# Separate step lists for sequences 0, 1 and 15 of a two-layer transformer kernel

## The chip, the cores and the metric

The kernel runs on one core of a Trainium2 chip. The core has five engines that work side by side and meet at semaphores: TensorE (PE, with its weight loads shown apart as PEld), VectorE (DVE), ScalarE (ACT), GpSimd (POOL) and SyncE (SP, which issues most of the DMAs here). The metric is the device time of one execution in microseconds.

## The reference, cut to what matters

The input is 16 sequences of 512 tokens with 256 channels. Two layers follow each other, each of an attention part and a feed-forward part, with a layernorm after each part.

- Layer 0, attention: queries, keys and values of 16 heads are mapped into latents of 32, rotated (rope), scored with a causal mask, put through a softmax, and weighted sums of the value latents go through two projections.
- Layer 0, feed-forward: inputs, hidden values and weights are quantized to FP4 in blocks of 16 and back; the form is silu(gate) * up, then down, with 704 hidden channels.
- Layer 1, attention: a recurrence over the 512 time steps, `state = tanh(state @ tanh(a) + x_t @ b)`, for all sequences at once.
- Layer 1, feed-forward: a gate and a squared relu of mixes of a token with the one before it.

```python
x = _layernorm(x + _L0_attn_ref(x, ...), axis=-1)
x = _layernorm(x + _L0_ffn_ref(x, ...), axis=-1)
x = _layernorm(x + _L1_attn_ref(x, ...), axis=-1)
x = _layernorm(x + _L1_ffn_ref(x, ...), axis=-1)
```

## The kernel before, in words

After a short preparation the kernel goes through the 16 sequences of layer 0 one after another (loop at L779). The recurrence of layer 1 needs all of them and comes last (L1118 and after).

**Slots.** A sequence is cut into 12 slots: 4 groups `g` of four heads by 3 blocks `n` of query rows. A slot issues the scores of four heads (`scores`, L516: matmuls into the four tiles `S`, then a masked pass on DVE that writes `p` and its extreme `nm`), and, for the slot before, four turns (`turn`, L555: transposes of `p` into `ps_pt`, copied by ACT to `pT`); the exponentials (`exponentials`, L544, ACT) run two heads behind. After a group's third block, `weighted` (L566) issues the 80 matmuls of `py`. In the second of a slot's four rounds `divide` (L597) turns the reciprocal sums (`ps_r`, copied to `rT`) and multiplies them into `yT`.

**Steps beside the scores.** All other work of layer 0 is cut into steps. A slot has eight half-slots, one before and one after each of its four turns, and each half-slot may issue some steps. An entry of the list `PLAN` (L632) such as `"U-1.2"` names a task, a sequence relative to the current one, and a part:

- `H` (L433): queries and keys of the heads, four steps per sequence. `V` (L415): values, two steps.
- `L` (L446): latents of one group, three steps: plain products (`ps_q`, `ps_k`), rotated ones (`ps_qs`, `ps_ks`), and the product `ps_qf` that ends in `qr`, which the scores read.
- `O` (L482): output projection, residual and layernorm, two steps. It waits until the last group of its sequence is divided.
- `Q` (L272): puts the quantization of 128 tokens into a queue whose pieces are issued one per half-slot (`vector_step`, L257), or at once when a step needs the result. The quantization (`fp4`, L181) is some nine DVE instructions and two on POOL, ending in `xq` or `hq`.
- `U` (L282): gate and up products of 128 tokens, three steps. The first transposes `xq` (`ps_xq`, copied to `xqT`); the other two are the products `pg` and `pu` and the silu. The last one queues the quantization of the hidden values.
- `D` (L313): down product of 128 tokens, two steps: transposes of `hq` (`ps_h`, copied by ACT to `hT`), and twelve matmuls into `ps_d` with residual, layernorm and the store.
- `W` (L217): quantizing and transposing the feed-forward weights, 30 steps, only beside sequence 0. `P`: a pause, which counts 0.5 of time and issues nothing.

`Beside` (L670) paces a list: the sum of `TIME` over its entries is spread evenly over the sequence's 96 half-slots, and an entry is issued when the credit is positive. A task is a generator, so an entry means "the next step of this task"; `"U-1.3"` in one list and `"U-2.3"` in the next go on with the same task.

**What sets the order.** PE's order is the program's, written by hand (`manual_schedule`). The instructions of DVE, ACT and POOL are ordered by a planner when the kernel is built; it may place an instruction before or after others of its engine as soon as its inputs and buffers are free by its own estimate, with the program's order as priority.[...]

**Buffers that matter below.** Two pools of PSUM banks (two and five) serve `S`, turns and steps; `py` has one bank. `hT`, `qc`, `qs` and `ks` have one buffer each; `xq`, `hq`, `xqT`, the quantization's scratch and the residual `x` have two.

**The lists before.** There is one list, `PLAN`. `plan(b)` (L647) drops entries whose sequence lies outside 0 to 15; at the last sequence it adds the leftovers of sequence 14 at the end; at sequence 0 it puts in the two `V` steps and spreads the 30 `W` steps over the rest of the list. After the last slot a list `FIRST` (L1085) does sequence 15's own feed-forward.

Of the kernel before, what the change touches and what calls it, by code (L numbers as in the profile page):

```python
# [19 lines left out]
P = 128  # L20
B, T, C = 16, 512, 256
NT = T // P
H, HD, L = 16, 16, 32
# [36 lines left out]
def tile_kernel(ctx: ExitStack, tc: tile.TileContext, I: dict, out: bass.AP):  # L60
# [87 lines left out]
    def mm(name):  # L148
        banks.append(banks.pop(0))
        return banks[-1].tile([P, 512], F32, tag="mm", name=name)  # L150
# [21 lines left out]
    def whole_steps(pieces):  # L172

        t = 0.0
        for dt, end in pieces:
            t += dt
            if end:
                yield t
                t = 0.0

    def fp4(dst, x, nb, rows=P):  # L181

        n = nb * 16
        sc = ffn.tile([P, 44], F32, tag="q_sc", name="q_sc", bufs=2)[:rows, :nb]  # L190
        inv = ffn.tile([P, 44], F32, tag="q_inv", name="q_inv", bufs=2)[:rows, :nb]
        q = ffn.tile([P, FF], F32, tag="q_q", name="q_q", bufs=2)[:rows, :n]
        m = ffn.tile([P, FF], F32, tag="q_m", name="q_m", bufs=2)[:rows, :n]

        def blocks(t):
            return t.rearrange("p (n k) -> p n k", k=16)

        def over(t):
            return t.unsqueeze(2).to_broadcast([rows, nb, 16])

        nc.vector.tensor_reduce(sc, blocks(x), AX.X, ALU.max, apply_absolute_value=True)
        nc.vector.tensor_scalar(sc, sc, 1.0 / 6.0, 1e-12, ALU.mult, ALU.max)
        nc.vector.reciprocal(inv, sc)
        nc.vector.tensor_scalar(inv, inv, 1.0 - 2.0**-23, None, ALU.mult)
        if n > C:
            yield
        nc.vector.tensor_tensor(blocks(q), blocks(x), over(inv), ALU.mult)
        yield
        nc.vector.tensor_scalar(m.bitcast(U32), q.bitcast(U32), 0x7F800000, None, ALU.bitwise_and)
        nc.vector.tensor_scalar(m, m, 1.0, 1.5 * 2.0**22, ALU.max, ALU.mult)  # L210
        if n > C:
            yield
        nc.vector.tensor_tensor(q, q, m, ALU.add)  # L213
        nc.gpsimd.tensor_tensor(q, q, m, ALU.subtract)  # L214
        nc.gpsimd.tensor_tensor(blocks(dst), blocks(q), over(sc), ALU.mult)

    def ffn_weights():  # L217

        for name, dst in (("w_gate", wgT), ("w_up", wuT)):
            for r in range(NFB):  # L220
                n = min(P, FF - r * P)
                w = ffn.tile([P, C], F32, tag="h", name="w", bufs=2)
                nc.sync.dma_start(w[:n, :], I[name][r * P : r * P + n, :])
                wq4 = ffn.tile([P, C], F32, tag="hq", name="wq4", bufs=2)
                for _ in fp4(wq4[:n, :], w[:n, :], C // 16, n):
                    pass
                yield 0.3
                ps = mm("ps_t")
                for cc in range(2):
                    nc.tensor.transpose(  # L230
                        ps[:, cc * P : cc * P + n], wq4[:n, cc * P : cc * P + P], ident[:n, :n]
                    )
                nc.scalar.copy(
                    dst[:, :, r * P : r * P + n],
                    ps[:, : 2 * P].rearrange("p (c n) -> p c n", c=2)[:, :, :n],
                )
                yield 1.2
        for r in range(2):
            w = ffn.tile([P, FF], F32, tag="h", name="w", bufs=2)
            nc.sync.dma_start(w, I["w_down"][r * P : r * P + P, :])  # L240
            wq4 = ffn.tile([P, FF], F32, tag="hq", name="wq4", bufs=2)
            for _ in fp4(wq4, w, FF // 16):
                pass
            yield 0.3
            for k0 in (0, 3):
                ps = mm("ps_t")
                for kb in range(k0, k0 + 3):
                    (of, n), at = PARTS[kb], (kb - k0) * P
                    nc.tensor.transpose(ps[:n, at : at + P], wq4[:, of : of + n], ident)
                    nc.scalar.copy(wdT[:n, kb, r * P : r * P + P], ps[:n, at : at + P])  # L250
                yield 1.5
# [30 lines left out]
    def ffn_up(b, j):  # L282
        vector_done(("x", b, j))
        xq = xq_of.pop((b, j))
        ps = mm("ps_xq")
        for cc in range(2):
            nc.tensor.transpose(ps[:, cc * P : cc * P + P], xq[:, cc * P : cc * P + P], ident)
        xqT = ffn.tile([P, 2, P], F32, tag="xqT", name="xqT", bufs=2)
        copier[0](xqT.rearrange("p c t -> p (c t)"), ps[:, : 2 * P])  # L289
        yield 0.3, True  # L290
        h = ffn.tile([P, FF], F32, tag="h", name="h", bufs=2)
        for f in range(2):
            fs = slice(f * 352, f * 352 + 352)

            th = ffn.tile([P, 352], F32, tag="th", name="th", bufs=2)
            for w in (wgT, wuT):
                ps = mm("pg" if w is wgT else "pu")
                for cc in range(2):
                    product_of[0](ps[:, :352], xqT[:, cc, :], w[:, cc, fs], cc == 0, cc == 1)
                    if cc == 0:  # L300
                        yield 0.6, False
                if w is wgT:
                    nc.scalar.activation(th, ps[:, :352], AF.Tanh, scale=0.5)
                    nc.vector.scalar_tensor_tensor(th, th, 1.0, ps[:, :352], ALU.add, ALU.mult)
                    yield 0.6, False
                else:
                    nc.vector.scalar_tensor_tensor(h[:, fs], th, 0.5, ps[:, :352], ALU.mult, ALU.mult)
            if f == 1:
                hq_of[b, j] = hq = ffn.tile([P, FF], F32, tag="hq", name="hq", bufs=2)
                queue(("h", b, j), fp4(hq, h, FF // 16))  # L310
            yield 0.6, True
# [29 lines left out]
    with ExitStack() as a:  # L341
# [44 lines left out]
        for i in range(2):  # L386
            nc.gpsimd.tensor_copy(bd["bdqs"][:, i::2], bd["bdq"][:, 1 - i :: 2])
            at = COLS["q2lb"][0]
# [3 lines left out]
        for i in range(2):  # L392
            at = COLS["cab"][0] + 2
# [222 lines left out]
        def pause(b):  # L616
# [10 lines left out]
        TASKS = {  # L627
            "L": latents, "H": heads, "V": values, "O": out_projection, "Q": quantize,
            "U": lambda b, j: whole_steps(ffn_up(b, j)), "D": lambda b, j: whole_steps(ffn_down(b, j)),
            "W": ffn_weights, "P": pause,  # L630
        }
        PLAN = [  # L632
            "L0.1", "L0.1", "U-2.3", "U-2.3", "H0", "H0", "O-1", "D-2.2", "L0.1", "D-2.2", "O-1",
            "V1", "L0.2", "L0.2", "L0.3", "Q-1.0", "L0.3", "Q-1.1", "U-1.0", "L0.2", "D-2.3",
            "U-1.1", "U-1.0", "U-1.0", "V1", "L0.3", "U-1.1", "Q-1.2", "H1", "U-1.2", "D-2.3",
            "Q-1.3", "U-1.2", "U-1.1", "U-1.2", "H1", "U-1.3", "D-1.0", "D-1.0", "D-1.1", "L1.0",
            "L1.0", "D-1.1", "L1.0",
        ]
        tasks = {}

# [5 lines left out]

        def plan(b):  # L647
            todo = []
            for entry in PLAN:
                c, *rest = entry[1:].split(".")  # L650
                c = b + int(c)
                if 0 <= c < B:
                    todo.append((entry[0], (c, *map(int, rest))))
            if b == B - 1:

                todo += [(e[0], (b - 1, int(e[-1]))) for e in PLAN if e[1:3] == "-2"]
            if b == 0:

                todo[2:2] = [("V", (0,))] * 2
                first = todo.index(("L", (0, 2))) + 3  # L660
                n = len(todo) - first
                for k in reversed(range(n)):
                    at = first + k + 1
                    todo[at:at] = [("W", ())] * ((k + 1) * 30 // n - k * 30 // n)
            return todo


# [2 lines left out]
        class Beside:  # L670
            def __init__(self, b):
                self.todo = plan(b)
                self.pace = sum(TIME[n] for n, _ in self.todo) / (4 * len(BLOCKS) * 8)
                self.left = 0.0
# [104 lines left out]
        with tc.manual_schedule(engines={mybir.EngineType.PE}):  # L779
# [4 lines left out]
            for slot in slots + [None]:  # L784
                if slot:
                    b, g, n = slot
# [281 lines left out]
    def beside(M):  # L1068

        todo = [("N", 1)] * 2 if M == 0 else []  # L1070
        for e in PERIOD:
            i = M + int(e[1:])
            if 0 <= i < T // TS:
                todo.append((e[0], i))
        return todo + LATER.get(M, [])
# [42 lines left out]
    with tc.manual_schedule(engines={mybir.EngineType.PE}):  # L1118
# [33 lines left out]
        todo, left, pace = [], 0.0, 0.0  # L1152
# [7 lines left out]
        for t in range(T):  # L1160
            if t % 16 == 0:
                for e in todo:
                    step(*e)
                todo, left = beside(t // 16), 0.0
# [5 lines left out]
            for g in range(2):  # L1170
                if us[g] is None or us[g][0] + us[g][1] == t:
                    t0, n = starts[g].pop(0)
# [6 lines left out]
            if t % 8 == 7:  # L1179
                at = t % 16 - 7  # L1180
# [113 lines left out]
```

## Time and profile before

| | |
|---|---|
| median of three runs | 2609.86 us (2609.65 to 2614.08) |
| the profiled execution | 2613.92 us, span 2612.1 us, mean granted PE clock 0.979 |
| busy, share of the span | PE 94%, PEld 66%, DVE 75%, ACT 62%, POOL 40% |
| first scores of sequence 0, 1, 2 | 32.6, 136.4, 259.7 us |
| one of sequences 2 to 14 | 107.5 to 109.0 us |
| first and last scores of sequence 15 | 1664.5, 1785.0 us |
| first step of the recurrence | 1864.4 us |

In rows of waits "PE ps_d L160 <- ACT hT L323: 2.7, 1, 2.7" means: PE stood still before an instruction of line 160 that writes `ps_d`, until ACT's instruction of line 323 on `hT` was done; 2.7 us in total, once, 2.7 at the longest. PE counts as busy while a matmul is on its way, so a small wait within a group of matmuls can hide there.

### The profile page before, as it was taken

The numbers are of one execution on the slowest core, as the hardware profiler recorded it, in microseconds if no ns is written. First come the engines' busy times: TensorE is split into PE (matmuls) and PEld (weight loads), VectorE is DVE, ScalarE is ACT, GpSimd is POOL, SyncE is SP. The second block draws the span as 40 slices with busy tenths as digits, with TensorE's granted clock in tenths as the row PEclk, the third lists the DMA queues.
The fourth block names the chain that finished last, engine by engine and source line by source line (L and its number), as shares of the span: only waits on it lengthen the run. The fifth ranks groups of instructions, "written<-read, shape, count | busy, mean of one in ns | idle before, by whom it ended". The sixth has DMA issues, their size and how long they took to land.

```text
span 2612.1 us, 73864 instructions
## 1 busy us (share of the span) xinstructions
PE 2451.8 (94%) x28802; PEld 1725.3 (66%) x28802; DVE 1946.2 (75%) x5621; ACT 1613.5 (62%) x5532; POOL 1044.0 (40%) x1649
## 2 busy tenths in 40 slices
PE   7788999999999999999999999987799999999997
PEld 4455666666666666666666666655577777777775
DVE  5865888788887888878888788875656666666665
ACT  4655666666766666666666666653266666666663
POOL 4322333333333333333333333333545555555553
PEclk9899999999999999999999999998899999999999
DMA  3000000000000000000000000000111111111100
GB/s 114 23 9 5 11 23 14 15 15 11 23 13 15 15 11 23 14 15 15 12 23 14 16 15 6 15 11 9 42 31 39 39 37 37 39 40 39 35 27 22
DMA packets 58016, 61.30 MB, mean 23 GB/s; under 512 B 7873, under 2 KB 53058, under 8 KB 57666
## 3 DMA queue, kind: packets, MB, share of 16 engines
q1 hardware_dynamic: 56802, 55.54, 6.9%
q8 instruction: 226, 3.70, 0.6%
q10 hardware_dynamic: 864, 1.05, 0.1%
q14 instruction: 124, 1.02, 0.1%
HBM read 39.79 MB, written 16.78 MB: 22 GB/s over the span
## 4 chain that ended last, share of the span: by engine, by line
PE 53%; DVE 30%; ACT 7%; POOL 4%; issue 4%; DMA 1%; SPq 1%; ACTq 0%; POOLq 0%; DVEq 0%
PE u L1053 7%; PE ps_pt L559 5%; DVE p L536 5%; PE S L524 5%; PE u L1013 4%; PE pg L160 3%; PE pu L160 3%; ACT p L549 3%; PE ps_d L160 3%; PE ps_h L439 3%; PE py L590 2%; PE ps_a L897 2%; PE ps_k L897 2%; PE ps_rr L897 2%; DVE q_q L213 2%
## 5 line engine op out<-in xcount | busy, mean ns | idle before, releaser
L549 ACT ACTIVATE p<-p,nm 128x512 f32<-128x512 f32 (+3 forms) x1024 | 569.4, 561 | 522.4 <-DVE nm L536 518.3
L1061 ACT ACTIVATE hist<-u 64x64 f32<-64x64 f32 x2048 | 445.6, 218 | 253.0 <-PE u L1053 183.3
L536 DVE CUSTOM_DVE_ANT_0 p<-S,mask 128x512 f32<-128x512 f32 (+3 forms) x1024 | 442.7, 483 | 71.5 <-PE S L524 71.4
L559 PEld LDWEIGHTS ps_pt<-ident,p 128*128 128x128 f32 x2560 | 299.0, 142 | 232.9 <-issue 89.1
L1053 PEld LDWEIGHTS u<-hist,ta 128*64 128x64 f32 x8176 | 363.3, 138 | 121.0 <-ACT hist L1061 41.7
L561 ACT COPY pT<-ps_pt 128x384 f32<-128x384 f32 (+1 forms) x768 | 370.9, 514 | 72.4 <-PE ps_pt L559 72.4
L559 PE MATMUL ps_pt<-ident,p 128*128 128x128 f32 x2560 | 394.0, 280 | 8.4 <-DVE nm L536 4.6
L1053 PE MATMUL u<-hist,ta 128*64 128x32 f32 x8176 | 384.5, 219 | 4.8 <-ACT hist L1061 4.6
L214 POOL TENSOR_TENSOR q_q<-q_q,q_m 128x256 f32<-128x256 f32 (+1 forms) x142 | 167.9, 1183 | 491.8 <-DVE q_q L213 486.7
L524 PE MATMUL S<-kc,qr 32*128 32x128 f32 (+3 forms) x2048 | 238.1, 474 | 11.6 <-ACT qr L478 9.5
L1013 PE MATMUL u<-xt,wb 128*64 128x64 f32 x4128 | 223.4, 230 | 3.5 <-issue 2.4
L549 ACT ACTIVATION_READ_ACCUMULATOR p<-p,nm 128x1 f32 x1024 | 198.5, 194 | 0.0
L160 PE MATMUL ps_d<-wdT,hT 128*128 128x256 f32 x732 | 180.2, 398 | 7.4 <-ACT hT L323 6.2
L160 PE MATMUL pg<-wgT,xqT 128*128 128x352 f32 x512 | 177.3, 469 | 7.9 <-ACT xqT L289 4.7
L160 PE MATMUL pu<-wuT,xqT 128*128 128x352 f32 x512 | 174.8, 464 | 0.0
L473 POOL TENSOR_TENSOR qc<-qc,qs 128x512 f32<-128x512 f32 x64 | 81.6, 1275 | 226.0 <-DVE qs L472 210.8
L1013 PEld LDWEIGHTS u<-xt,wb 128*64 128x64 f32 x4128 | 165.2, 139 | 9.2 <-issue 3.0
L590 PEld LDWEIGHTS py<-pT,vpad 128*32 128x32 f32 x5120 | 138.6, 110 | 39.7 <-issue 32.1
L524 PEld LDWEIGHTS S<-kc,qr 32*128 32x128 f32 x2048 | 111.0, 184 | 79.0 <-issue 37.1
L590 PE MATMUL py<-pT,vpad 128*32 128x128 f32 x5120 | 160.5, 274 | 2.7 <-ACT pT L561 2.4
L160 PEld LDWEIGHTS ps_d<-wdT,hT 128*128 128x128 f32 x732 | 141.5, 200 | 30.4 <-ACT hT L323 11.5
L1187 POOL COPY c<-hist 64x256 f32<-64x256 f32 x256 | 111.3, 435 | 65.6 <-ACT hist L1061 56.1
(164 smaller groups left out, 4536.0 us busy)
## 6 DMA issues: line engine op xcount, KB each, us to landing
xT<-in_xT_dram SPq DMA_DIRECT2D x16, 512.0 KB
x<-in_x_dram SPq DMA_DIRECT2D x16, 512.0 KB
xs<-x SPq DMA_DIRECT2D x64, 128.0 KB
x<-xs SPq DMA_DIRECT2D x32, 256.0 KB
xm<-xs SPq DMA_DIRECT2D x32, 256.0 KB
out_dram<-o SPq DMA_DIRECT2D x64, 128.0 KB
w<-in_w_down_dram SPq DMA_DIRECT2D x2, 352.0 KB
w<-in_w_gate_dram SPq DMA_DIRECT2D x5, 128.0 KB
```

The lines of the kernel that those rows point to most:

```text
L160: nc.tensor.matmul(dst, left, right, start=start, stop=stop)
L214: nc.gpsimd.tensor_tensor(q, q, m, ALU.subtract)
L524: nc.tensor.matmul(S[h][:, at : at + w], q[rs, i * P : i * P + P], k[rs, :w], start=True, stop=True,)
L536: nc.vector.tensor_tensor_reduce(out=p[:, own], in0=S[h][:, own], in1=mask[:, T - (i + 1) * P :], scale=1.0, scalar=-MASKED, op0=ALU.add, ...
L549: nc.scalar.activation(p[:, own], p[:, own], AF.Exp, bias=nm[:, u : u + 1], scale=-1.0, accum_out=sum_of[b, g][:, cb, half, h : h + 1],)
L559: nc.tensor.transpose(ps[:, at : at + P], p[:, at : at + P], ident)
L561: nc.scalar.copy(pT[:, :w], ps[:, :w])
L590: nc.tensor.matmul(py[q * 32 : q * 32 + 32, PLACE[i][1], :], vpad[b % 2][:, j, g * 4 + h, :], pt, start=j == 0 and h % 2 == 0, stop=j == i ...
L897: nc.tensor.matmul(dst[cs], left[:, cs], right, start=first, stop=not first)
L1013: nc.tensor.matmul(u[rs, k, par:n:2, bs : bs + 16], wb[:, g * 2 + k, par, half, rs], xt[:, g, at : at + n - par : 2, :], start=par == 0 an ...
L1053: nc.tensor.matmul(into[cs, :, c, :], ta[:, t % 2, g * 2 + k, cs], own[:, :, c, :], start=False, stop=True, skip_group_check=True,)
L1061: nc.scalar.activation(state[g][rs, :, r * 32 : r * 32 + 32].rearrange("p k (s b) -> p k s b", s=2), u[rs, :, t - t0, :] .rearrange("p k ( ...
```

## The change

The middle list keeps its entries; four of its steps change places. Sequences 0, 1 and 15 get lists of their own, so `plan` no longer drops or adds anything. The new lists hold the same steps as before, in another order, plus one pause in the lists of 0 and 1 and five in that of 15. Some `D` and `U` steps of sequences 13 and 14 beside sequence 15 now interleave with each other.

```diff
-            "W": ffn_weights, "P": pause,
+            "W": lambda b: ffn_weights(), "P": pause,
         }
         PLAN = [
-            "L0.1", "L0.1", "U-2.3", "U-2.3", "H0", "H0", "O-1", "D-2.2", "L0.1", "D-2.2", "O-1",
-            "V1", "L0.2", "L0.2", "L0.3", "Q-1.0", "L0.3", "Q-1.1", "U-1.0", "L0.2", "D-2.3",
+            "L0.1", "L0.1", "U-2.3", "U-2.3", "H0", "H0", "O-1", "D-2.2", "L0.1", "O-1", "V1",
+            "D-2.2", "L0.2", "L0.2", "L0.3", "Q-1.0", "L0.3", "Q-1.1", "L0.2", "U-1.0", "D-2.3",
             "U-1.1", "U-1.0", "U-1.0", "V1", "L0.3", "U-1.1", "Q-1.2", "H1", "U-1.2", "D-2.3",
             "Q-1.3", "U-1.2", "U-1.1", "U-1.2", "H1", "U-1.3", "D-1.0", "D-1.0", "D-1.1", "L1.0",
             "L1.0", "D-1.1", "L1.0",
         ]
+        PLAN_0 = [
+            "H0", "L0.1", "H0", "V0", "V0", "L0.1", "L0.2", "W0", "V1", "L0.1", "L0.2", "V1",
+            "L0.3", "L0.2", "W0", "L0.3", "W0", "W0", "W0", "H1", "L0.3", "W0", "W0", "W0", "H1",
+            "W0", "W0", "W0", "W0", "W0", "W0", "W0", "L1.0", "W0", "W0", "W0", "W0", "L1.0", "W0",
+            "W0", "W0", "W0", "W0", "W0", "L1.0", "W0", "W0", "W0", "W0", "W0", "P0",
+        ]
+        PLAN_1 = [
+            "H0", "H0", "L0.1", "L0.1", "O-1", "O-1", "L0.1", "L0.2", "L0.2", "Q-1.1", "V1", "L0.3",
+            "Q-1.0", "U-1.0", "U-1.1", "U-1.0", "P0", "U-1.0", "V1", "L0.2", "L0.3", "U-1.1",
+            "Q-1.2", "U-1.1", "U-1.2", "L0.3", "D-1.0", "H1", "Q-1.3", "H1", "L1.0", "D-1.0",
+            "U-1.2", "L1.0", "D-1.1", "U-1.2", "U-1.3", "L1.0", "D-1.1",
+        ]
+        PLAN_15 = [
+            "L0.1", "U-2.3", "U-2.3", "H0", "H0", "L0.1", "O-1", "D-2.2", "L0.1", "P0", "D-2.3",
+            "L0.2", "D-2.2", "L0.3", "L0.2", "O-1", "Q-1.0", "U-1.0", "L0.2", "L0.3", "U-1.0", "P0",
+            "P0", "Q-1.1", "U-1.0", "L0.3", "U-1.1", "U-1.1", "D-2.3", "Q-1.2", "Q-1.3", "P0",
+            "U-1.2", "D-1.0", "U-1.3", "U-1.2", "P0", "U-1.1", "U-1.2", "D-1.0", "U-1.3", "U-1.3",
+            "D-1.1", "D-1.1", "D-1.3", "D-1.2", "D-1.3", "D-1.2",
+        ]
...
-            for entry in PLAN:
+            for entry in {0: PLAN_0, 1: PLAN_1, B - 1: PLAN_15}.get(b, PLAN):
                 c, *rest = entry[1:].split(".")
-                c = b + int(c)
-                if 0 <= c < B:
-                    todo.append((entry[0], (c, *map(int, rest))))
-            if b == B - 1:
-
-                todo += [(e[0], (b - 1, int(e[-1]))) for e in PLAN if e[1:3] == "-2"]
-            if b == 0:
-
-                todo[2:2] = [("V", (0,))] * 2
-                first = todo.index(("L", (0, 2))) + 3
-                n = len(todo) - first
-                for k in reversed(range(n)):
-                    at = first + k + 1
-                    todo[at:at] = [("W", ())] * ((k + 1) * 30 // n - k * 30 // n)
+                todo.append((entry[0], (b + int(c), *map(int, rest))))
             return todo
```

## Prediction

> **What bounds the kernel now.** I read the slices of the page first, then busy times by stage, then who TensorE waits for in each stage, and last single instructions at the longest stalls.
>
> ```profile
> ## 2 busy tenths in 40 slices
> PE   7788999999999999999999999987799999999997
> ...
> PEclk9899999999999999999999999998899999999999
> ```
>
> TensorE (PE) is full nearly everywhere. The holes are at both ends of the attention part: slices 0 to 3 and 26 to 28. PEclk dips where PE has holes. I cut the span at the first score matmul of sequences 0, 1, 2, 4, 5, 15 and at the end of the scores:
>
> ```profile
> 32.60:136.40 103.80, 85.71 (x647) 51.13 (x647) 72.81 (x235) 69.29 (x215) 33.61 (x40) 0.89 0.12 35
> 136.40:259.70 123.30, 102.40 (x799) 65.16 (x798) 77.18 (x245) 67.32 (x196) 29.50 (x34) 0.95 0.02 8
> 259.70:367.20 107.50, 105.74 (x848) 70.85 (x848) 88.50 (x266) 73.25 (x224) 37.55 (x45) 1.00 0.05 15
> 475.20:583.00 107.80, 105.84 (x848) 70.91 (x849) 88.94 (x266) 70.95 (x213) 37.25 (x45) 1.00 0.05 16
> 1664.50:1785.00 120.50, 104.86 (x825) 70.66 (x825) 84.68 (x251) 65.56 (x190) 34.48 (x42) 0.94 0.04 11
> 1785.00:1864.40 79.40, 52.35 (x326) 36.78 (x324) 54.10 (x142) 15.12 (x45) 32.30 (x42) 0.83 0.07 22
> ```
>
> The columns are the length, then busy PE, PEld, DVE, ACT, POOL, and the clock. A middle sequence takes 107.5 to 109.0 us with PE idle for about 2: PE sets the pace, at full clock. Sequence 1 has fewer matmuls (799 against 848) and takes 123.3 us, 20.9 of them idle; sequence 15 takes 120.5 with 15.6 idle; sequence 0 takes 103.8 with 18.1 idle and 647 matmuls. No engine is full there. So these three are bound by the order of the list: PE meets a step whose input is still being made. The longest such waits of PE in sequence 0, in 1, and in 15 to its last step:
>
> ```profile
> PE ps_t L249 <- POOL wq L215: 4.8, 1, 4.8
> PE ps_t L249 <- ACT wdT L250: 4.7, 8, 1.5
> PE ps_pt L559 <- DVE nm L536: 3.1, 1, 3.1
> ```
>
> ```profile
> PE pg L160 <- ACT xqT L289: 3.2, 1, 3.2
> PE pg L160 <- DVE nm L536: 3.2, 1, 3.2
> PE ps_d L160 <- ACT hT L323: 2.7, 1, 2.7
> PE ps_o L491 <- DVE yT L611: 2.6, 1, 2.6
> ```
>
> ```profile
> PE ps_xq L287 <- POOL xq L215: 7.2, 1, 7.2
> PE ps_h L321 <- POOL hq L215: 4.0, 1, 4.0
> PE ps_d L160 <- ACT hT L323: 3.3, 1, 3.3
> ```
>
> The timeline of the 4.0 us shows what a quantization costs from end to end:
>
> ```profile
> 1784.09 0.89 DVE L201 TENSOR_REDUCE q_sc<-h 128x44 f32<-128x704 f32 x1
> ...
> 1789.23 1.68 POOL L214 TENSOR_TENSOR q_q<-q_q,q_m 128x704 f32<-128x704 f32 x1 [15.54 <-DVE q_q L213]
> ...
> 1790.99 1.38 POOL L215 TENSOR_TENSOR hq<-q_q,q_sc 128x704 f32<-128x704 f32 x1
> ...
> 1792.43 1.54 PE L321 MATMUL ps_h<-ident,hq 128*128 128x128 f32 x6 [3.95 <-POOL hq L215]
> ```
>
> From 1784.09 to 1792.37 is 8.3 us on DVE and POOL; PE had too little between to cover it.
>
> **What the Trainium skill says.** "TensorE: Matmul & The Clock Gate", Part 1 (the HAM clock gate): PE drops to half clock after an idle window of about 3.4 us and needs a busy one to recover. The trace agrees: four `pg` matmuls take 1.35 us at 1744.7 and 2.71 us at 1819.3, behind a stall of 10.2 us. So a stall costs itself plus slow matmuls behind it. The same page, Architectural detail, says that ACT and DVE are strictly first in, first out[...]; the trace agrees at 1710 to 1714, where DVE sits 3.3 us in front of `yT` although a ready quantization stands behind it. The page "PSUM — Partial Sum Buffer", Specifications (TRN2), gives eight banks; the code spends two and five of them on scores, turns and steps and one on `py`. That they can run out is seen below, at `ps_k`.
>
> **The change part by part.** I place steps by walking each list at its pace (sum of TIME over 96 half-slots) and write slot.half, so 6.2 is slot 6, half-slot 2. A half-slot is 1.1 to 1.3 us (a stage's length over 96). No instruction is added or removed: PE, DVE, ACT, POOL and DMA work are the same, and a pause issues nothing. Issues on SP follow their steps; DMA is 2 to 12% busy in these stages, nothing on the path. Only what stands between a producer and its reader moves. The planner lets DVE, ACT and POOL run ahead of a step's place (the first quantization of a weight starts at 14.5 us, long before its place in slot 3), so mostly PE's place of the reader counts.
>
> *Sequence 15.* (a) `U14.2`'s transpose goes from 6.2 to 6.7, five half-slots, at the middle's 1.12 us 5.6 us of other work: the 7.2 becomes about 2; -5. (b) The last part of `U14.3` goes from 10.3 to 9.6, its `D` from 11.4 to 10.7. The distance stays nine half-slots, but they now hold the second half of `D14.1` (12 matmuls, 2.7), `py` (2.3), sixteen transposes (2.2), the scores (0.9) and 1.6 of other transposes: 9.7 against the chain of 8.3, with up to 3.6 us of DVE's other work mixed in (four score passes of 0.55, one layernorm of 1.4): -2.5. (c) The two halves of `D14.1` go from neighbours (9.1, 9.2) to 10.2, 10.3 with about 1 us of transposes between: -1. (d) DVE's lateness around slot 8 (1.6 + 1.0 + 0.4): -1. (e) Half clock fills 20 us here; with half of that gone, at 70% busy, 10 x 0.5 x 0.7 = 3.5; I take -2.5. (f) New: `D13.3` begins (2.4) before `D13.2` ends (2.7), and `D14.2` before `D14.3`, on the single buffer `hT`: the copy (0.87) waits for 12 matmuls; +1 each, and +1 for its bank. Sum -9, bounds -16 and +5.
>
> *Sequence 1.* (a) `U0.2`'s transpose and first product, at 6.5 and 6.6, part to 6.4 and 8.7: -3.2. (b) `D0.0`'s halves, 9.1 and 9.2, part to 6.7 and 8.1: -2.7. (c) `L1.2` and `L1.3`, packed into 2.2 to 3.3 (waits of 1.3 and 1.1), spread to 6.5: -2. (d) `L2.0` ends at 10.5 instead of 11.3: the next scores' 1.6 falls to the middle's 0.5; -1. (e) Waits on `nm` (3.2, 1.1, 1.0) are DVE's lateness; -1. (f) 12.5 us of half clock shrink; -2. (g) `O0` stays right behind the division: 0. (h) New: `U0.0`'s transpose and product become neighbours (3.0, 3.1), where such neighbours cost 3.2 above; +2. `L1.3` starts at 2.6, but its `qc` (one buffer) is free only when `L1.2` ends, at 4.6 instead of 3.3: a bank is held some 11 half-slots longer; +1. Sum -9, bounds -17 and +6.
>
> *Sequence 0.* (a) Quantization of `w_down` and its transposes, both at 10.0, go to 9.7 and 10.1: 4.8 falls by 3 half-slots at most; -2. (b) `wdT` (4.7) is a transpose waiting for the copy of the one before in its bank: 0. (c) The `L` steps spread from slot 2 (eight pairs) over slots 1 to 4, the weights in slot 5 thin out: the 3.1 and the slow scores in slots 3 and 6 (2.7 and 2.1 against 1.1 us); -3. (d) Clock, 21.9 us at half: -1. Sum -6, bounds -13 and +5.
>
> *Sequences 2 to 14.* `O`'s second half goes from 3.2 to 2.5, `V` from 3.4 to 2.7, `D-2.2`'s second half from 2.5 to 3.1, `U-1.0`'s transpose from 4.3 to 4.5, `L.2`'s end from 4.4 to 4.3. In slot 3 `ps_o` held its bank from 505.8 to 509.2 behind DVE's four score passes and `ps_k` started 0.8 late. That 0.8 goes; slot 2 becomes fuller, +0.5. -0.3 x 13 = -4, bounds -1.5 and +3 each (-20 and +39). `U-1.0`'s copy is covered by six transposes of `D-2.3`, two turns and two more transposes, some 2.3 us.
>
> After 1785 us nothing moves; the end of sequence 15 only shifts it. Sum: -9 - 9 - 6 - 4 = -28. The profiled execution took 2613.92 us (span 2612.1 and 1.8 around it), the median of the runs is 4 us lower: 2609.86 - 28 = **2582**.
>
> **Rivals.** *A middle list that waits* (slower). ACT takes `xqT`'s copy late because exponentials ahead of it wait for DVE: ACT waits 418 us for `nm` in the middle. `U-1.0`'s product then stands as in sequence 1, 3.2 us. It counts thirteen times: from 24 / 13 = 1.8 us per sequence the gain of the three lists is used up; 3.2 gives 2609.86 - 24 + 42 = 2628. Against it: the cover of 2.3 us. *Stalls that move* (no change): DVE and ACT are ordered anew by the planner, and what one stall loses the next regains, as the old list's `D` and `U` of sequence 15 queue for the same DVE; 2605 to 2615. *All to the floor* (faster still): without idle time and half clock sequence 15 would take about 105, 1 about 106, 0 about 92: -15 - 17 - 12 - 4 = -48: 2562. For it: besides PE no engine is over 71% busy there. Against it: DVE and ACT must then never be late.
>
> **How the numbers follow.** Forecast 0.53 (own range 2566 to 2598), floor 0.16, no change 0.12, waiting middle 0.19. Within 0.2% (5 us) is about what a measurement of this kernel can't tell from no change. Faster 0.69, same 0.12, slower 0.19. From 2552 to 2626 the range takes the forecast, no change, most of the floor and half of the slower case.
>
> **What would show it.** Right: sequences 0, 1 and 15 at about 98, 114 and 112 us by the first scores; `ps_xq <- xq` in 15 under 3 us, `pg <- xqT` and `ps_d <- hT` gone from 1; fewer half-clock windows; a middle sequence at 107.3. Wrong: a middle sequence over 109 us with a new row in PE's waits, or `xq` and `hq` waits of the old size at new places.

## The result, and the profile after

The changed kernel takes 2582.46 us (median; 2580.31 to 2582.77), beside 2611.97 us for the kernel before, measured together: ratio 0.9884, 95% interval 0.9867 to 0.9901, about 30 us faster. The profiled execution has a span of 2581.0 us (before 2612.1) and a mean PE clock of 0.983 (before 0.979).

The slices of the page after, busy tenths and granted clock:

```profile
PE   8789999999999999999999999996899999999997
PEclk9899999999999999999999999998899999999999
```

The hole of three slices behind sequence 15 has become two; the first slices have hardly changed. The windows of the kernel after, cut at the same places (first scores of sequences 0, 1, 2; of 4 and 5; first and last of 15; first step of the recurrence). Columns: length, then busy PE, PEld, DVE, ACT, POOL, the clock, DMA:

```profile
31.55:130.30 98.75, 82.52 (x650) 51.10 (x650) 69.83 (x234) 68.62 (x213) 34.19 (x39) 0.90 0.12 37
130.30:241.40 111.10, 99.06 (x798) 63.71 (x797) 76.68 (x239) 65.33 (x194) 29.60 (x34) 0.95 0.02 8
458.00:566.00 108.00, 105.98 (x848) 70.78 (x849) 89.11 (x266) 71.07 (x213) 37.46 (x45) 1.00 0.05 16
1652.10:1762.50 110.40, 100.29 (x825) 66.76 (x826) 88.16 (x259) 65.48 (x190) 37.12 (x44) 0.98 0.03 11
1762.50:1833.60 71.10, 47.36 (x322) 33.34 (x322) 50.62 (x136) 14.69 (x45) 29.23 (x40) 0.88 0.08 27
```

Beside the windows of before, with the whole middle (sequences 2 to 14) from its first to its last first score:

| stage | before | after | difference | foretold |
|---|---|---|---|---|
| start, to the first scores | 32.6 | 31.6 | -1.0 | 0 |
| sequence 0 | 103.8 | 98.7 | -5.1 | -6 |
| sequence 1 | 123.3 | 111.1 | -12.2 | -9 |
| sequences 2 to 14 | 1404.8 | 1410.7 | **+5.9** | -4 |
| sequence 15 to its last scores | 120.5 | 110.4 | -10.1 | -9, with the next row |
| from there to the recurrence | 79.4 | 71.1 | -8.3 | |
| recurrence and after | 747.7 | 747.3 | -0.4 | 0 |

So the forecast met the time while one of its terms had the wrong sign and another was half of what came: the middle became slower by 5.9 where -4 stood, and sequence 15 with what follows gained 18.4 where -9 stood. That the sum came out at 2582 is luck: the two errors are of nearly the same size and of opposite sign.

In sequence 15 PE's idle time (length less busy) fell from 15.6 to 10.1 and behind it from 27.1 to 23.7, together by 8.8. The other 9.6 lie in PE's *busy* time (104.86 + 52.35 = 157.2 before, 147.6 after) for nearly the same matmuls (1151 and 1147): most of that is the clock, 0.94 and 0.83 before, 0.98 and 0.88 after. The trace's clock stands at half for 41 us of these two stages before and for 20 after, and PE is busy in 26.6 and 10.0 us of that time. Half of the difference, 8.3 us, is an estimate of what the clock gave back (the four `pg` of the prediction take 1.35 us at full clock and 2.71 at half).

In sequence 1 idle time fell by 8.9 and busy time by 3.3, in sequence 0 by 1.9 and 3.2. There the mean clock hardly moved (0.95 in both, and 0.89 to 0.90), and the same count gives the clock only 0.6 and 0.9 of the busy time. No run shows what the rest is; small waits within a group of matmuls count as busy.

PE's longest waits after, by stage. Sequence 0:

```profile
PE ps_t L249 <- ACT wdT L250: 5.7, 8, 2.0
PE ps_t L230 <- POOL wq L215: 2.7, 1, 2.7
PE ps_t L249 <- POOL wq L215: 2.5, 1, 2.5
```

The wait of 4.8 for `w_down` became 2.5, and the 3.1 in front of a turn shrank to 0.7; a wait of 2.7 for another weight is new. Sequence 1:

```profile
PE ps_xq L287 <- POOL xq L215: 4.4, 1, 4.4
PE ps_o L491 <- DVE yT L611: 2.0, 1, 2.0
PE ps_pt L559 <- DVE nm L536: 1.7, 2, 1.2
```

`pg <- xqT` (3.2), `pg <- nm` (3.2) and `ps_d <- hT` (2.7) are gone; in their place stands a new 4.4 before the transpose of `U0.0`, which the new list puts at slot 3.0. Sequence 15, to its last scores:

```profile
PE ps_pt L559 <- DVE x L331: 1.9, 1, 1.9
PE pg L160 <- ACT xqT L289: 1.4, 1, 1.4
PE ps_d L160 <- ACT hT L323: 1.4, 1, 1.4
```

The 7.2 before `ps_xq` is gone from this table (0.4 is left in the single waits), the 3.3 before `ps_d` is 1.4. Behind the last scores:

```profile
PE ps_xq L287 <- POOL xq L215: 10.2, 1, 10.2
PE ps_h L321 <- POOL hq L215: 6.1, 1, 6.1
```

Before, the second row was "10.1, 2, 6.1": the 4.0 of sequence 14's last `hq` has gone, and the two waits of sequence 15's own feed-forward (10.2 and 6.1) stand unchanged, as nothing there was moved.

### The profile page after: what moved, and what is told of

Read it like the earlier page. It is cut to its first block, busy times and chain, and to the rows that moved or that the text cites. A ratio compares the mean times of both kernels' runs of the same rounds, so it can differ in the third digit from the quotient of the medians.

```text
span 2581.0 us, 73861 instructions
## 1 busy us (share of the span) xinstructions
PE 2438.0 (94%) x28802; PEld 1715.8 (66%) x28802; DVE 1946.9 (75%) x5621; ACT 1615.6 (63%) x5532; POOL 1048.2 (41%) x1649
## 4 chain that ended last, share of the span: by engine, by line
PE 58%; DVE 27%; ACT 7%; POOL 4%; issue 3%; DMA 0%; ACTq 0%; POOLq 0%; DVEq 0%; SPq 0%
PE u L1060 7%; PE ps_pt L559 6%; PE S L524 5%; DVE p L536 5%; PE u L1020 4%; PE pg L160 4%; PE pu L160 3%; PE py L590 3%; ACT p L549 3%; PE ps_h L439 3%; PE ps_d L160 2%; PE ps_a L904 2%; PE ps_k L904 2%; ACT pT L561 2%; PE ps_q L457 2%
## 5 line engine op out<-in xcount | busy, mean ns | idle before, releaser
L160 PE MATMUL ps_d<-wdT,hT 128*128 128x256 f32 x732 | 169.5, 381 | 2.2 <-ACT hT L323 2.2
L160 PEld LDWEIGHTS ps_d<-wdT,hT 128*128 128x128 f32 x732 | 134.8, 191 | 19.6 <-ACT hT L323 3.1
L84 POOL TENSOR_SCALAR ve<-mv 128x1 f32<-128x1 f32 (+1 forms) x160 | 32.8, 205 | 264.5 <-DVE mv L92 234.7
```

The costliest lines, as they stand in the source:

```text
L160: nc.tensor.matmul(dst, left, right, start=start, stop=stop)
```

## Experiments: which list does it

**The lists without the middle, and the middle alone.**

`lists_only`, against the kernel after:

```diff
-            "L0.1", ..., "O-1", "D-2.2", "L0.1", "O-1", "V1",
-            "D-2.2", "L0.2", "L0.2", "L0.3", "Q-1.0", "L0.3", "Q-1.1", "L0.2", "U-1.0", "D-2.3",
+            "L0.1", ..., "O-1", "D-2.2", "L0.1", "D-2.2", "O-1",
+            "V1", "L0.2", "L0.2", "L0.3", "Q-1.0", "L0.3", "Q-1.1", "U-1.0", "L0.2", "D-2.3",
```

> The three own lists with the middle list of before. Theory A, the stages add as the two traces show them (sequence 0: -5.1 us, 1: -12.2, 2 to 14: +5.9, 15 with what follows it: -18.7): about 37 us faster than before, 2575 us, and a middle sequence back at 107.5 to 109.0 us, so 6 us faster than the whole change. Theory B, the middle's +0.45 us per sequence comes from what the new list of sequence 1 leaves behind, or from the planner, not from the four moved steps: no faster than the whole change, 2582 us, with middle sequences at 108.0 to 109.6 us.

`middle_only`: sequences 0, 1 and 15 as before, the new middle for the others.

```diff
-            for entry in PLAN:
+            for entry in MIDDLE if 2 <= b < B - 1 else PLAN:
```

> Only the middle list is new; sequences 0, 1 and 15 are as before. Theory A: +6 us against before (+0.45 us in each of thirteen sequences), 2618 us. Theory B: no difference, within 2 us. The prediction on record had -4 us, with 0.8 us per sequence gone at ps_k in slot 3 and 0.5 us added in slot 2.

Measured: `lists_only` 2580.9 us, ratio 0.9874 (0.9856 to 0.9892). `middle_only` 2620.89 us, ratio 1.0022 (1.0012 to 1.0031). The three lists hold the whole gain, and the middle's four moves cost: sequences 2 to 14 take 1409.9 us in `middle_only` and 1410.7 after, 1405.8 in `lists_only` and 1404.8 before. That is 0.4 us per sequence, thirteen times, and the interval of `middle_only` leaves out no change. The whole time of `lists_only` was foretold at 2575 and isn't told apart from that of the change (2582.46); that the middle went back to its old length is read from the stage.

**One list at a time.** `list15_only` and `list1_only` give the new list to that sequence and leave all others as before:

```diff
+            if b in {15: PLAN_15}:
+                for entry in {15: PLAN_15}[b]:
+                    c, *rest = entry[1:].split(".")
+                    todo.append((entry[0], (b + int(c), *map(int, rest))))
+                return todo
```

> Only the list of sequence 15 is new. Theory A: -19 us, 2593 us, with 110 us from its first to its last scores and 71 us from there to the first step of the recurrence. Theory B, part of the gain hangs on the new end of the middle list: -10 to -14 us. The prediction on record had -9 us.

> Only the list of sequence 1 is new. Theory A: -12 us, 2600 us, sequence 1 at 111 us. Theory B, sequence 1 profits from what the new list of sequence 0 leaves ready at its start: -6 us or less, sequence 1 at 117 us or more. The prediction on record had -9 us.

Measured: 2599.03 us, ratio 0.9941 (0.9922 to 0.996), and 2601.61 us, ratio 0.9944 (0.9923 to 0.9965): some 15 us each, and with a few for sequence 0, whose list wasn't run alone, they add up to the 33 of `lists_only`. `list1_only` is as its theory A has it; `list15_only` lies between its two theories. The gains sit where the list is: in `list15_only` sequence 15 takes 110.1 and what follows 73.2 (before 120.5 and 79.4), with sequence 1 at 125.1; in `list1_only` sequence 1 takes 112.1, with 121.1 and 79.5 at the other end. What one stall loses is not regained at another, so the lists don't share a bottleneck.

The size of a stage at the ends is known to some microseconds only. Over the profiles of all kernels here, sequence 1 takes 123.3 to 128.1 us with its old list and 109.1 to 112.1 with its new one, and sequence 0 103.8 to 105.5 and 98.6 to 102.4. Sequence 15 with what follows takes 199.8 to 200.6 with the old list and 181.6 to 185.7 with the new one. The gains are clear of this; the -12.2 and the -18.4 of one pair of profiles are not exact.

## Experiments: why the middle lost

Four moves are in the middle list. `middle_o_v` makes two of them (`O` and `V` ahead of `D-2.2`'s second half), `middle_l_u` the other two (`L.2`'s end ahead of `U-1.0`'s transpose). Both have the three lists.

```diff
 middle_o_v, against lists_only
-            ..., "D-2.2", "L0.1", "D-2.2", "O-1", "V1", ...
+            ..., "D-2.2", "L0.1", "O-1", "V1", "D-2.2", ...
 middle_l_u, against lists_only
-            ..., "Q-1.1", "U-1.0", "L0.2", "D-2.3",
+            ..., "Q-1.1", "L0.2", "U-1.0", "D-2.3",
```

> Three own lists, and of the middle list's moves only the first: the second half of O and V forward, the second half of D-2.2 behind them. Theory A, this move alone makes the middle slower, because O's work on DVE now stands ahead of slot 3's score passes: slots 2 and 3 together +0.5 to +0.6 us per sequence against the old middle list, slot 4 unchanged at 10.45 us, 7 us slower than the three lists alone (about 2588 us). Theory B, it also brings the gain seen in slot 4: slot 4 at 10.15 us, +0.25 us per sequence, +3 us.

> Three own lists, and of the middle list's moves only the second: the last step of L.2 ahead of the transpose of U-1.0. Theory A: slot 4 falls from 10.45 to 10.15 us on its own, 4 us faster than the three lists alone and 6 us faster than the whole change (about 2577 us). Theory B: slot 4 stays at 10.45 us and the kernel equals the three lists alone (2581 us).

Measured: `middle_o_v` 2588.35 us, ratio 0.9907 (0.9888 to 0.9927); `middle_l_u` 2573.81 us, ratio **0.9849** (0.9834 to 0.9863). The second has the lowest time of the study and beats both kernels of the case: its interval lies just below that of the change (0.9867 to 0.9901).

Slot by slot the two can be told apart. Mean over sequences 2 to 14, us, from one slot's first score matmul to the next slot's; the other nine slots differ by 0.12 us at most, slot 0 of `middle_o_v` and of before apart (12.05 and 11.86, the others 11.93):

```
              slot 2   slot 3   slot 4   whole sequence
before          8.72    11.53    10.45       108.06
lists_only      8.73    11.54    10.44       108.13
after           9.23    11.59    10.15       108.52
middle_o_v      9.23    11.58    10.51       108.91
middle_l_u      8.73    11.56    10.09       107.84
```

`O` and `V` forward: slot 2 grows by 0.50 and slot 3 doesn't shrink (with small changes elsewhere the sequence grows by 0.78). `L` before `U`: slot 4 loses 0.35 in the mean, 0.42 to 0.68 in nine of the thirteen sequences and nothing in the other four. What the second does is one line. The timeline of the kernel before, PE in slot 4 of sequence 4 (start, length, operation, and in brackets the idle time ahead of it and its releaser):

```profile
518.34 0.38 PE L287 MATMUL ps_xq<-ident,xq 128*128 128x128 f32 x2
519.03 1.10 PE L476 MATMUL ps_qf<-qc,w 128*128 128x512 f32 x2 [0.31 <-ACT pT L561]
```

`ps_xq` stands ahead of `ps_qf`, which then waits 0.31 until ACT has emptied a bank of turns. In `middle_l_u` the order is reversed and neither waits:

```profile
500.32 1.02 PE L476 MATMUL ps_qf<-qc,w 128*128 128x512 f32 x2
501.18 0.60 PE L559 MATMUL ps_pt<-ident,p 128*128 128x128 f32 x4
501.62 0.38 PE L287 MATMUL ps_xq<-ident,xq 128*128 128x128 f32 x2
```

In the four sequences without a gain (5, 7, 12 and 14) it is `ps_xq` that waits with the old order, and `ps_qf` as long with the new one. Slots 2 to 4 came as theory A of each run had them.

Why slot 3 didn't shrink is on DVE. Slot 3 lost PE work: it had `O` and `V` (1.89 us each) and now has `D-2.2`'s twelve matmuls (2.76), 1.0 less. The timeline of the kernel before, DVE, sequence 4, whose slot 3 begins with the scores at 502.48:

```profile
505.01 0.65 DVE L536 CUSTOM_DVE_ANT_0 p<-S,mask 128x512 f32<-128x512 f32 x1
...
508.23 0.69 DVE L536 CUSTOM_DVE_ANT_0 p<-S,mask 128x512 f32<-128x512 f32 x1
508.84 0.09 DVE L536 DVE_READ_ACCUMULATOR2_ANT nm<- 128x1 f32 x1
```

The first of the four score passes comes 2.5 us after the first score matmul, the third ends at 508.12 and the fourth at 508.93. The products of `L.2` come right behind them:

```profile
508.17 1.12 PE L457 MATMUL ps_q<-heads,bdq 64*128 64x512 f32 x2
508.98 1.12 PE L457 MATMUL ps_k<-heads,bdk 64*128 64x512 f32 x2
```

In the kernel after slot 3 begins at 485.79:

```profile
485.09 0.68 DVE L497 TENSOR_TENSOR x<-ps_o,x 128x512 f32<-128x512 f32 x1
...
485.89 0.75 DVE L91 BATCH_NORM_STATS2 bnst<-x 128x6 f32<-128x256 f32 x2
...
488.24 1.50 DVE L502 TENSOR_SCALAR x<-x,mv,rstd 128x256 f32<-128x256 f32 x2 [0.87 <-POOL rstd L86]
489.66 0.68 DVE L536 CUSTOM_DVE_ANT_0 p<-S,mask 128x512 f32<-128x512 f32 x1
```

`O`'s residual and layernorm (L497 to L502) now stand ahead of the score passes, with 0.87 of pure waiting for POOL's `rstd` and a final pair that takes 1.50. The first score pass comes 3.9 us after the first score matmul. `L.2`'s products wait for the passes to free the `S` banks, so they come hardly earlier than before although PE has less to do until then (`ps_q` 5.56 us after the slot's first score matmul, 5.69 before):

```profile
489.84 1.11 PE L559 MATMUL ps_pt<-ident,p 128*128 128x128 f32 x6
491.35 1.12 PE L457 MATMUL ps_q<-heads,bdq 64*128 64x512 f32 x2 [0.40 <-DVE nm L536]
492.16 1.12 PE L457 MATMUL ps_k<-heads,bdk 64*128 64x512 f32 x2
```

Which pass a product waits for follows from the code: `mm` (L148) hands out the seven banks in turn, so a product gets the bank that was handed out seven before. Counted so, `ps_q` and `ps_k` get the banks of the third and fourth `S` of their slot before. After, with one step less between, they get those of the second and third, whose passes end at 491.30 and 492.11. All four start 0.05 us behind their pass. So the products now wait for one pass less, but the passes come 1.3 us later.

To see whether the culprit is `O`'s DVE work or the thinner slot, two more orders, both on `middle_l_u`:

```diff
 o_forward
-            ..., "D-2.2", "L0.1", "D-2.2", "O-1", "V1", ...
+            ..., "D-2.2", "L0.1", "O-1", "D-2.2", "V1", ...
 v_forward
-            ..., "D-2.2", "L0.1", "D-2.2", "O-1", "V1", ...
+            ..., "D-2.2", "L0.1", "V1", "D-2.2", "O-1", ...
```

> Three own lists and the middle list with L.2 ahead of U-1.0; in addition only O's second half moves forward, to just before the second half of D-2.2, and V stays behind both. Theory A, O's own DVE work ahead of slot 3's score passes is what cost time in the whole change: it costs here too, slots 2 and 3 +0.5 us per sequence, 6 us slower than without. Theory B, slot 3 then had too little PE work between its scores and L.2's products to cover DVE's score passes (2.8 us of D instead of 3.8 of O and V): here D and V lie between, 4.7 us, so the loss is gone, slots 2 and 3 at 20.2 us or less.

> Three lists of their own, middle list of middle_l_u with V ahead of D-2.2's second half and O's second half last ("L0.1", "V1", "D-2.2", "O-1"). By the pacing this puts V at 2.6, D-2.2's second half at 2.8 and O at 3.5, exactly o_forward with O and V exchanged. Theory A (the harm comes from O's vector work, rstd and layernorm, placed ahead of slot 3's score passes; O now behind them): a middle sequence near that of middle_l_u, 107.8 to 108.3 us mean, whole 2572 to 2580. Theory B (the harm is TensorE's, slot 3 is left with too little to do before L's products, whichever step comes forward): slots 2 and 3 grow as in o_forward, 109.5 to 110.5 us per sequence, whole 2595 to 2610.

Measured: `o_forward` 2605.34 us, ratio 0.9964 (0.9953 to 0.9976); `v_forward` 2575.48 us, ratio 0.9861 (0.9844 to 0.9878). Neither theory of `o_forward` foretold this: the pacing put `D-2.2`'s second half at the end of slot 2, so slot 3 didn't get the work that theory B counted on. `v_forward` is the cleaner test. The pacing gives both the same places, with `O` and `V` exchanged, and PE the same 121 matmuls in slot 3. One is slower by 30 us, 2.2 us per sequence (110.1 and 107.88). PE in slot 3 of `o_forward`, then of `v_forward`, sequence 4:

```profile
491.79 1.14 PE L524 MATMUL S<-kc,qr 32*128 32x512 f32 x8
492.86 0.88 PE L559 MATMUL ps_pt<-ident,p 128*128 128x128 f32 x6
495.26 1.99 PE L421 MATMUL ps_v<-wv,xT 128*128 128x256 f32 x8 [1.52 <-DVE x L331]
```

```profile
484.04 1.14 PE L524 MATMUL S<-kc,qr 32*128 32x512 f32 x8
485.11 0.88 PE L559 MATMUL ps_pt<-ident,p 128*128 128x128 f32 x6
485.82 1.89 PE L491 MATMUL ps_o<-cpT,yT 128*128 128x256 f32 x8
```

With `O` in front, DVE's `x <- ps_d` (L331), which frees the bank that `V` needs, waits behind `O`'s layernorm. A table of eight of the kernels, mean over sequences 2 to 14: the time from slot 3's first score matmul to DVE's first score pass, and how many of the 64 instructions that end `O`'s layernorm (L502) took about 0.79 us where 0.41 is usual:

```
              first score pass   L502 at 0.79 us   slots 2 + 3
before                  2.54                 0         20.25
lists_only              2.53                 0         20.27
middle_l_u              2.54                 0         20.29
v_forward               1.86                 0         20.32
middle_only             3.86                26         20.80
middle_o_v              3.87                26         20.81
after                   3.88                26         20.82
o_forward               4.01                26         22.67
```

The four kernels with `O` in front have both marks and the longer slots, the four others neither. That `O`'s vector work and not `V` is the cause is shown by the exchange. How the delay divides among its residual, its wait for `rstd` and its slowed last pair no run separates. How far it hurts differs with what PE has beside it: 0.55 us in slots 2 and 3 with `D` in slot 3 (after), 2.4 without (`o_forward`), both against `lists_only`.

## Experiments: how the moves in sequence 15 act

Two of the moves of sequence 15's list, each alone in the kernel before. `u142` puts `U14.2`'s transpose behind `Q14.3`, and the first step of `D14.0` behind it:

```diff
+            if b == B - 1:
+                for name, j, behind in (("U", 2, ("Q", (b - 1, 3))), ("D", 0, ("U", (b - 1, 2)))):
+                    todo.remove((name, (b - 1, j)))
+                    at = todo.index(behind) + 1
+                    todo[at:at] = [(name, (b - 1, j))]
```

> The list of before; in sequence 15 alone the transpose of U14.2 and the first step of D14.0 move back behind Q14.3, the quantization stays where it was. Theory A, as predicted, PE's place of the reader decides: PE's wait for xq falls from 7.2 to at most 2 us, and sequence 15 with what follows is 5 us shorter. Theory B, DVE and ACT are as late as before and the wait turns up again at the next steps: slot 6 shorter, slots 7 to 9 longer, 0 to 2 us in all.

`end15` puts `U14.3`'s last two steps ahead of `D14.1`:

```diff
+            if b == B - 1:
+                up, first = [("U", (b - 1, 3))] * 2, todo.index(("D", (b - 1, 1)))
+                todo = [e for k, e in enumerate(todo) if k < first or e != up[0]]
+                todo[first:first] = up
```

> The list of before; in sequence 15 alone the last two steps of U14.3 move ahead of both steps of D14.1. Theory A, as predicted, the wait of 4.0 us for hq is covered by D14.1: gone, with the half clock behind it, 4 to 6 us, all of it between the last scores and the recurrence (79.4 us before). Theory B, D14.1 or the end's D steps wait in its place: under 2 us.

Measured: 2606.26 us, ratio 0.997 (0.9963 to 0.9977), and 2605.7 us, ratio 0.9972 (0.9963 to 0.9981). PE's longest waits in sequence 15 of `u142`:

```profile
PE ps_d L160 <- DVE nm L536: 4.3, 1, 4.3
PE ps_xq L287 <- POOL xq L215: 4.0, 1, 4.0
```

The 7.2 fell only to 4.0, and a new 4.3 stands at the next `D`: sequence 15 became 4.9 shorter, and what follows 1.9. In `end15` the 4.0 before `hq` behind the last scores is gone (1.2 more stand before a `ps_d`): sequence 15 takes 120.5 as before, and what follows 73.2 in place of 79.4, 6.2 less for a wait of 4.0. The windows of `end15`, sequence 15 and what follows:

```profile
1668.00:1788.50 120.50, 103.51 (x825) 69.34 (x825) 87.77 (x258) 65.44 (x190) 37.52 (x44) 0.96 0.03 10
1788.50:1861.70 73.20, 48.92 (x328) 34.30 (x324) 50.95 (x136) 14.71 (x46) 29.27 (x40) 0.88 0.08 26
```

Of the 6.2, 3.4 are PE's busy time (52.35 to 48.92) at a clock of 0.88 in place of 0.83. The other 2.8 are idle time. So taking away a wait of 4.0 shortened the stage by more than the wait, since the matmuls ran faster. As for the expectations: in `u142` the stage gained what theory A said, with the wait only in part gone and a new one as theory B said; `end15` is as its theory A has it. By stage the two alone bring 6.8 and 6.2 of the 18.4 that the whole list brings; the rest comes from moves that weren't tried alone. Both profiles also differ from that of before where nothing was edited (the recurrence 3 us shorter in both, as it is in `v_forward` and `u00_later`, and sequence 1 4.8 us longer in `u142`), which no run here explains; so the whole times, 7 to 8 us better, aren't these stages alone.

**The price of the clock by itself.** `filled` is `middle_l_u` with matmuls into a bank that nobody reads, 20 ahead of sequence 15's own feed-forward and 11 ahead of its first `D`. It adds work and leaves none out.

```diff
+        def fill(n):
+            ps = mm("ps_fill")
+            for _ in range(n):
+                nc.tensor.matmul(ps[:, :C], ident, wdT[:, 0, :], start=True, stop=True)
+
+        fill(20)
+        for k, e in enumerate(FIRST):
+            if k == FIRST.index("D0"):
+                fill(11)
```

> Three own lists and the middle list with only L.2 ahead of U-1.0 (2573.8 us); added are 20 and 11 matmuls that nobody reads, in the two longest waits of PE after the last sequence (10.2 us before ps_xq, 6.1 us before ps_h). It measures what the half clock behind a stall costs by itself. Theory A, half clock lengthens what follows: with PE kept busy the first pg and pu and the later ps_d run at full clock, 3 to 4 us shorter from the last scores to the recurrence (71.5 us before). Theory B, the path there runs over DVE and POOL, and slow matmuls hide beside it: 0 to 1 us. If the added matmuls are in the way themselves, it is slower.

Measured: 2578.59 us, ratio 0.9865 (0.9845 to 0.9886), no gain on `middle_l_u`. In the stage itself the theory of the clock holds: the windows from the last scores to the recurrence, of `middle_l_u` and then of `filled`:

```profile
1755.30:1826.90 71.60, 47.87 (x328) 33.71 (x324) 50.76 (x136) 14.70 (x45) 29.30 (x40) 0.88 0.08 27
```

```profile
1751.10:1818.90 67.80, 57.86 (x389) 43.30 (x386) 49.19 (x131) 14.76 (x45) 28.34 (x39) 1.00 0.09 28
```

The clock goes to 1.00 and the stage from 71.6 to 67.8. But PE then reaches the recurrence's preparation before POOL has made its inputs, and its first steps wait. Waits from 1810 to 1835 us in `filled`:

```profile
PE ps_xn L883 <- POOL xn L867: 11.5, 3, 7.9
```

In `middle_l_u` this row has 2.1 in four waits before the recurrence and 1.8 once in it. In both kernels POOL's queue holds the pieces of sequence 15's `hq` (1.7 and 1.5 to 1.9 us each in `filled`) between those of `xn`. That `xn` is late because of them is a reading of the queue and wasn't tried. The recurrence and after take 753.7 us in place of 747.2. So full clock was worth 3.8 us in that stage, and was given back in the next.

**The new wait in sequence 1.** `u00_later` puts `V` and `L.2`'s third step of that list ahead of `U0.0`'s transpose, on `middle_l_u`:

```diff
-            "Q-1.0", "U-1.0", "U-1.1", "U-1.0", "P0", "U-1.0", "V1", "L0.2", "L0.3", "U-1.1",
+            "Q-1.0", "V1", "L0.2", "U-1.0", "U-1.1", "U-1.0", "P0", "U-1.0", "L0.3", "U-1.1",
```

> middle_l_u with one edit in the list of sequence 1: V's second half and L.2's third step go ahead of U0.0's first step, so that its transpose stands at 3.5 instead of 3.1. Theory A (the 4.4 us that TensorE waits for xq in slot 3 of sequence 1 is a transpose placed too early): the wait falls to 1 us or less, sequence 1 is 3 to 4 us shorter (about 107 to 108), whole 2570 to 2571. Theory B (DVE and POOL are simply behind there; the wait moves to the next reader): a wait of 2 to 4 us at another step of slots 3 to 5, sequence 1 at 110 to 112, whole 2573 to 2576.

Measured: 2576.62 us, ratio 0.9866 (0.9851 to 0.9881), beside 0.9849 (0.9834 to 0.9863) for `middle_l_u`. Sequence 1 takes 111.5 us (111.2 in `middle_l_u`). The 4.4 is gone from its waits, and the first row is now:

```profile
PE pg L160 <- DVE nm L536: 2.2, 1, 2.2
```

It is two slots later. The 4.4 itself isn't fixed: in four other profiles with the list unedited it is 2.8, and sequence 1 takes 109.1 or 109.2. One of them, `v_forward`, agrees with `u00_later` in slots 0 to 2 to 0.1 us. Beside it slot 3 is 1.0 us shorter and slot 4 1.4 shorter, but slot 5 is 4.2 longer, at a clock of 0.87 in place of 1.00. Theory B held in this try: a later transpose only moves the wait.

## Why the prediction was right or wrong

*The time* (2582, measured 2582.46) is right as a sum and not in its parts: two errors of size 10 cancelled by luck.

*Sequence 15* foretold -9, came -18.4. The mechanism was right, the lists of waits confirm (a), (b) and (c): 7.2 became 0.4 (foretold about 2), 4.0 went, 3.3 became 1.4. The terms of idle time, (a) to (d) and (f), sum to -6.5; idle time fell by 8.8. (a) alone can't be had by its own move: in `u142` the wait was still 4.0, and 4.3 came up at the next `D`. The list brought it to 0.4 by moving the steps around it as well. What (f) cost can't be told apart; rows of 1.9 before a turn and 1.2 before a `pu` are new. The mis-sized term is (e), the half clock: -2.5 foretold, and 9.6 less busy time measured, some 8.3 of it by the clock. That half of it would go was right. But the working counted 20 us of half clock, up to 1803 us, and left out the 20 from there to the recurrence ("nothing moves"): 41 us became 20. `end15` shows the same: a wait of 4.0 gone, and 3.4 of busy time with it.

*Sequence 1* foretold -9, came -12.2. (a), (b) and (e) went as said: the three waits are gone. (g) held: `ps_o <- yT` stays at 2.0. (h) is the term that was undersized: +2 was put there for `U0.0`, and its transpose waits 4.4 (2.8 in some other profiles with this list). (f) foretold -2 from half clock, which only went from 12.5 to 11.0 us; busy time fell by 3.3 for the most part by something else, which stays open. With (h) at 4.4 at least, idle time fell by 8.9 all the same: the gains (a) to (e), 10 in the working, were about 13.

*Sequence 0* foretold -6, came -5.1: (a) 2.3 off the `w_down` wait (foretold 2), (b) `wdT` still there (5.7, before 4.7), (c) the 3.1 before a turn down to 0.7. (d), the clock, is about right: 0.9 of the 3.2 by which busy time fell. Idle time fell by only 1.9, as `wdT` waits 1.0 longer and a wait of 2.7 at another weight is new. So the sum is near and its parts are not.

*The middle* foretold -4, came +5.9, in spite of a fair reading of the slot. The step that failed is "That 0.8 goes". It took `ps_k`'s lateness for `ps_o`'s bank, held behind DVE's four score passes. But `ps_k` starts 0.05 us behind the fourth score pass: it waited for the passes themselves, which free the `S` banks, and it never gets the bank of `ps_o`. The 0.81 us between `ps_q` and `ps_k` stand after the change too. Moving `O` forward puts its own layernorm ahead of the passes on DVE's queue, and they come 1.3 us later. The other half of that sentence, slot 2 fuller by 0.5, was exact. The rival of a middle that waits was right in sign and wrong in its place and price: not `U-1.0`'s product on `xqT` (that move gains 0.29 per sequence), but `O`'s vector work, 0.55 to 0.8 per sequence.

*The rivals.* Stalls that move: refuted for the three lists by the separate runs, whose gains add up, but true of single moves, `u142` in part and `u00_later` whole. All to the floor: not reached; PE still idles 16.2, 12.0 and 10.1 us in sequences 0, 1 and 15. Of the marks, 98, 114 and 112 us came as 98.7, 111.1 and 110.4, half clock in the four stages at the ends fell from 75 to 52 us, and the middle sequence at 107.3 didn't come (108.5).

## What to carry to other kernels

A step that is moved on TensorE takes its vector tail along: look at what then stands ahead of the next urgent instruction on VectorE's queue, and count the waits of that tail on a third engine. A stall of TensorE is priced with the slow matmuls behind it, and all of them count, up to the next stage (here about as much as the stall again in sequence 15 and what follows, but hardly anything in sequence 1). The gain stays only where the engines that feed what comes next keep up. Where terms repeat thirteen times, half a microsecond of sign error weighs as much as a whole stall elsewhere: take the one slot apart instruction by instruction before giving it a sign.

## What the runs showed of the hardware

- VectorE's subtract-and-multiply of 128x256 (L502) takes 0.41 us, and about 0.79 when a GpSimd instruction on two tensors runs beside it from its start (to 0.01 us): in sequence 4 of the kernel after it runs from 488.24 to 489.04 and from 488.96 to 489.74, beside GpSimd instructions from 488.17 to 488.89 and from 488.97 to 489.59. These two rows of GpSimd's timeline are the ones beside it:

```profile
488.17 0.73 POOL L214 TENSOR_TENSOR q_q<-q_q,q_m 128x256 f32<-128x256 f32 x1
488.97 0.62 POOL L215 TENSOR_TENSOR xq<-q_q,q_sc 128x256 f32<-128x256 f32 x1
```

  The Trainium skill, "SBUF — State Buffer", section "SBUF: two separate sides", says that VectorE and GpSimd share a port pair which one of them holds for a whole instruction. The trace agrees: each of the two ends 0.15 us after the GpSimd instruction beside it. It happened in exactly 26 of 64 cases (two in each of the thirteen middle sequences) in all four kernels with `O` in front, and in none in the other four. Of the other 38 in the kernel after, 36 have no GpSimd instruction beside them and take 0.41 or less. One starts 0.16 us ahead of a GpSimd instruction and takes 0.41, and one takes 3.67 beside four GpSimd memsets.
- Some slots repeat over the thirteen middle sequences to within 0.02 us: in the kernel after, slot 2 takes 9.22 or 9.23 us and the first score pass of slot 3 comes 3.87 or 3.88 us after the scores. There a change of 0.3 us is read from one profile, where the whole time of a run spreads over several us. It doesn't hold for every slot: slot 4 of the kernel before takes 9.96 to 11.19 us, so it has to be compared sequence by sequence.
